# Aggregation by graph: 64-row TensorE tiles in pairs instead of one block-diagonal 128-row matmul

## Chip, cores, metric

One core of one Trainium2 chip. The metric is the device time of one launch in microseconds (us). Every ratio is between kernels run in the same rounds on the same chip. A difference between two experiments can cross rounds and chips; the medians of the kernel before in all these rounds lie between 2644.3 and 2645.0.

## The reference, cut to what matters

128 graphs of 64 nodes with 256 features pass through four layers. The first is a five-step gated network, which is most of the time; each of its steps sums the neighbours' features (`agg`):

```python
A = (adj != 0).astype(x.dtype)                    # (128, 64, 64)
for l in range(5):
    m = jnp.einsum('bnd,de->bne', h, weight[l])
    agg = jnp.einsum('bij,bid->bjd', A, m)        # the aggregation
    h = _gru_cell(agg, h, w_ih, w_hh, b_ih, b_hh)
# layer 1: neighbour sum again, then a two-layer MLP; layers 2 and 3: other uses of adj
```

The kernel aggregates `h` first and multiplies by the weights after, which is the same sum. All arithmetic is f32.

## The kernel before

Two graphs are stacked on the 128 partitions and four such pairs ("blocks", NB = 4) make a group, so there are 16 groups. The adjacency of a block is a 128 x 128 tile `ed[:, b, :]` with one graph in each diagonal quarter and zeros elsewhere. One aggregation handles 128 of the 256 features: four matmuls into one PSUM bank (PSUM holds matmul results; the program has eight banks) and one copy of the bank by ScalarE. There are 16 groups x 6 (five steps and layer 1) x 2 feature halves = 192 aggregations.

```python
# layer 0, step l, feature half c   (cut)
ps = bank("ps_agg")
for b in range(NB):
    def one(ps=ps, b=b, c=c, l=l, hr=hr):
        h = hr[:, b, :] if l else xt[:, b, c * P:(c + 1) * P]
        matmul(ps[:, b * P:(b + 1) * P], h, ed[:, b, :], 0, 1)   # out, stationary, moving
    pe(128, one, [ps], [hr if l else xt, ed])
act(512, lambda ps=ps, a=agg[c]: nc.scalar.copy(a.tile(), ps.tile()), [agg[c]], [ps])
```

`pe`, `act` and `flow.op` only record an operation with a guessed duration. At the end, `Flow.issue` puts the operations of up to five streams (set-up and groups) in one static order by list scheduling, so that other groups' work fills the waits of one. The guesses therefore decide the order, but they are not times.

Of the kernel before, what the change touches and what calls it, by code (L numbers as in the profile page):

```python
# [16 lines left out]
P = 128  # L17
# [25 lines left out]
class Op:  # L43
    __slots__ = ("eng", "us", "run", "stream", "n", "need", "then", "at", "bufs", "opens")

    def __init__(self, eng, us, run, stream, n):
        self.eng, self.us, self.run, self.stream, self.n = eng, us, run, stream, n
        self.need, self.then, self.at, self.bufs, self.opens = 0, [], 0.0, (), None


class Flow:
# [18 lines left out]
    def op(self, eng, us, run, w=(), r=()):  # L70
        o = Op(eng, us, run, len(self.streams) - 1, len(self.ops))
        before = set()
        for accesses, writes in ((r, False), (w, True)):
            for a in accesses:
                b, part = a if isinstance(a, tuple) else (a, None)
                if not b.uses and b.slot is not None:
                    ring = self.slots.setdefault(b.slot[0], deque(maxlen=b.slot[1]))
                    if len(ring) == b.slot[1]:
                        before.update(u[0] for u in ring[0].uses)
                    ring.append(b)  # L80
                for u, p, wr in b.uses:
                    if (wr or writes) and (p is None or part is None or p == part):
                        before.add(u)
        before.discard(o)
        touched = set()
        for accesses, writes in ((r, False), (w, True)):
            for a in accesses:
                b, part = a if isinstance(a, tuple) else (a, None)
                if b.bank and not b.uses:
                    o.opens = b  # L90
                b.uses.append((o, part, writes))
                if b not in touched:
                    touched.add(b)
                    b.left += 1
        o.bufs = [b for b in touched if b.bank]
        o.need = len(before)
        for u in before:
            u.then.append(o)
        self.ops.append(o)

    def issue(self):
        clock = dict.fromkeys(self.AHEAD, 0.0)
        queues = [{e: deque(o for o in ops if o.eng == e) for e in clock} for ops in self.streams]
        banks = [0.0] * BANKS
        left = sum(len(ops) for ops in self.streams)
        first = 0
        while left:
            best = None
            for s in range(first, min(first + 5, len(queues))):
                for e, q in queues[s].items():  # L110
                    opened = False
                    for i, o in zip(range(self.AHEAD[e]), q):
                        if o.opens is not None and (opened or not banks):
                            opened = True
                            continue
                        if o.opens is not None and o.need:
                            opened = True
                        if o.need:
                            continue
                        t = max(clock[e], o.at, banks[0] if o.opens is not None else 0.0)  # L120
                        if best is None or (t, s, o.n) < best[0]:
                            best = (t, s, o.n), o
            (t, s, _), o = best
            queues[s][o.eng].remove(o)
            o.run()
            end = t + o.us
            clock[o.eng] = end
            if o.opens is not None:
                banks.pop(0)
            for u in o.then:  # L130
                u.need -= 1
                u.at = max(u.at, end + (self.HOP if u.eng != o.eng else 0.0))
            for b in o.bufs:
                b.left -= 1
                if not b.left:
                    banks.append(end + self.HOP)
                    banks.sort()
            left -= 1
            while first < len(queues) and not any(queues[first].values()):
                first += 1  # L140
# [3 lines left out]
def kernel(  # L144
# [29 lines left out]
    nc = tc.nc  # L174
    B, N, D = x.shape
# [3 lines left out]
    NB = 4  # L179
# [13 lines left out]
    flow = Flow()  # L193
    quads = [slice(t * N, (t + 1) * N) for t in range(2)]
# [5 lines left out]
    def bank(name):  # L200
        return Buf(lambda: psum.tile([P, 512], F32, tag="bank", name=name), bank=True)
# [7 lines left out]
    def matmul(o, lhsT, rhs, k, nk):  # L209
        nc.tensor.matmul(o, lhsT, rhs, start=(k == 0), stop=(k == nk - 1))  # L210

    def pe(n, run, w, r):
        flow.op("PE", {512: 0.86, 256: 0.46, 257: 0.46, 128: 0.33}.get(n, 0.3), run, w, r)
# [7 lines left out]
    def act(n, run, w, r):  # L221
        flow.op("ACT", 0.16 + 0.001 * n, run, w, r)
# [122 lines left out]
    for l in range(L):  # L345
        ps = bank("ps_wmT")
# [8 lines left out]
        for k in range(KD):  # L355
            for j, n in ((0, 2 * D), (2 * D, D)):
                ps = bank("ps_wmih")
# [38 lines left out]
    def group(g):  # L396
# [12 lines left out]
        def rows_T(tag, name, bufs, src):  # L409
# [7 lines left out]
                act(R, lambda ps=ps, k=k: nc.scalar.copy(dst[k].tile(), ps.tile()), [dst[k]], [ps])  # L417
            return dst

        def layer_norm(y, name):  # L420
            st, mv = tiny("st", (P, NB, 6)), tiny("mv", (P, NB, 2))
            ve, rstd = tiny("ve"), tiny("rstd")
            for b in range(NB):
                dve(256, lambda b=b: nc.vector.bn_stats(st[:, b, :], y[:, b, :]), [(st, b)], [(y, b)])  # L424
                dve(4, lambda b=b: nc.vector.bn_aggr(mv[:, b, :], st[:, b, :]), [(mv, b)], [(st, b)])  # L425
            pool(0.23, lambda: nc.gpsimd.tensor_scalar(ve.tile(), mv[:, :, 1], LN_EPS, None, OP.add), [ve], [mv])  # L426
            pool(1.04, lambda: nc.gpsimd.tensor_tensor(rstd.tile(), ve.tile(), m_half, OP.pow), [rstd], [ve])  # L427
            o = rows("xn", f"x_{name}", 2)
            for b in range(NB):
                dve(256, lambda b=b: nc.vector.tensor_scalar(  # L430
                    o[:, b, :], y[:, b, :], mv[:, b, 0:1], rstd[:, b:b + 1], OP.subtract, OP.mult),
                    [(o, b)], [(y, b), mv, rstd])
            return o
# [3 lines left out]
        xt = loads.pop(g)  # L437
        araw, ed = a_raw[s], edge[s]
        for t in range(2):
            q = quads[t]  # L440
            dve(128, lambda q=q: nc.vector.tensor_scalar(ed[q, :, q], araw[q, :, q], 0.0, None, OP.not_equal),
                [(ed, t)], [(araw, t)])
        ps = bank("ps_adjT")
# [8 lines left out]
        hr = None  # L452
        for l in range(L):
            agg = [u("agg", f"agg{l}_{c}", bufs=2) for c in range(KD)]
            for c in range(KD):
                if l:
                    hr = u("hr", f"hr{l}_{c}", (P, NB, P), 2)
                    ps = bank("ps_hr")
                    for b in range(NB):
                        turn(lambda ps=ps, b=b, h=hT[c]: nc.tensor.transpose(  # L460
                            ps[:, b * P:(b + 1) * P], h[:, b * P:(b + 1) * P], ident.tile()), [ps], [hT[c]])
                    act(512, lambda ps=ps, hr=hr: nc.scalar.copy(hr.tile(), tiles_of(ps.tile())), [hr], [ps])
                ps = bank("ps_agg")
                for b in range(NB):
                    def one(ps=ps, b=b, c=c, l=l, hr=hr):
                        h = hr[:, b, :] if l else xt[:, b, c * P:(c + 1) * P]
                        matmul(ps[:, b * P:(b + 1) * P], h, ed[:, b, :], 0, 1)
                    pe(128, one, [ps], [hr if l else xt, ed])
                act(512, lambda ps=ps, a=agg[c]: nc.scalar.copy(a.tile(), ps.tile()), [agg[c]], [ps])  # L469
            hN = [u("hT", f"hT{l}_{c}", bufs=4) for c in range(KD)]  # L470
            for c in range(KD):
                def gate(i, sides, name):
# [38 lines left out]
        for h in range(NB // 2):  # L511
            ps = bank("ps_h")
            for k in range(KD):
                for j in range(2):
                    b = 2 * h + j
# [3 lines left out]
            for j in range(2):  # L519
                b = 2 * h + j  # L520
# [5 lines left out]
        for t in range(2):  # L526
            q = quads[t]
# [3 lines left out]
        x1 = layer_norm(y0, "n0")  # L531


        agg = [u("agg", f"aggm{c}", bufs=2) for c in range(KD)]
        for c in range(KD):
            ps = bank("ps_agg1")
            for b in range(NB):
                pe(128, lambda ps=ps, b=b, c=c: matmul(
                    ps[:, b * P:(b + 1) * P], x1[:, b, c * P:(c + 1) * P], ed[:, b, :], 0, 1), [ps], [(x1, b), ed])
            act(512, lambda ps=ps, a=agg[c]: nc.scalar.copy(a.tile(), ps.tile()), [agg[c]], [ps])  # L540
        hid = [u("hT", f"hid{c}", bufs=4) for c in range(4)] + [u("hr", f"hid{4 + c}", (P, 3 * D), 2) for c in range(2)]
        hid += [u(t, f"hid_{t}") for t in "AB"]
        hid = hid[:KH]
# [2 lines left out]
        for c in range(KH):  # L546
            ps = bank("ps_hid")
# [15 lines left out]
        ps = bank("ps_ss")  # L563
# [13 lines left out]
        for c in range(KH):  # L577
# [4 lines left out]
            b, i = (gt[0], None) if c % 3 == 0 else (gt[1], c % 3 - 1)  # L582
# [7 lines left out]
        for h in range(NB // 2):  # L590
            ps = bank("ps_o1")
            for j in range(2):
                b = 2 * h + j
# [4 lines left out]
            for j in range(2):  # L598
                b = 2 * h + j
# [40 lines left out]
        for h in range(NB // 2):  # L640
            for j in range(2):
                b = 2 * h + j
                pe(256, lambda b=b, j=j, ps=sup[h]: matmul(
                    ps[:, j * D:(j + 1) * D], adjT[:, b, :], tan[:, b, :], 0, 1), [sup[h]], [adjT, (tan, b)])
            for j in range(2):
                b = 2 * h + j
# [110 lines left out]
```

## Time and profile before

| | before |
|---|---|
| time, median (range), 3 runs | 2644.6 us (2644.04 to 2645.34) |
| PE busy / span of the profiled run | 2563.2 / 2642.7 us |
| pairs of weight load and matmul | 8770, of them 1536 in the aggregation |
| mean granted TensorE clock | 0.988 |

An f32 matmul stands in the trace as two pairs of LDWEIGHTS (on PEld; it loads the stationary operand) and MATMUL (on PE; it streams the columns of the moving operand). A matmul's listed duration (276 ns) is its latency; its pace is the distance from one start to the next. Since PE is busy 97% of the time, a change is judged by what it does to PE's pace.

### The profile page before, as it was taken

The numbers are of one execution on the slowest core, as the hardware profiler recorded it, in microseconds if no ns is written. First come the engines' busy times: TensorE is split into PE (matmuls) and PEld (weight loads), VectorE is DVE, ScalarE is ACT, GpSimd is POOL, SyncE is SP. The second block draws the span as 40 slices with busy tenths as digits, with TensorE's granted clock in tenths as the row PEclk, the third lists the DMA queues.
The fourth block names the chain that finished last, engine by engine and source line by source line (L and its number), as shares of the span: only waits on it lengthen the run. The fifth ranks groups of instructions, "written<-read, shape, count | busy, mean of one in ns | idle before, by whom it ended". The sixth has DMA issues, their size and how long they took to land.

```text
span 2642.7 us, 24329 instructions
## 1 busy us (share of the span) xinstructions
PE 2563.2 (97%) x8770; PEld 1448.5 (55%) x8770; DVE 1312.2 (50%) x3191; ACT 933.4 (35%) x1637; POOL 321.5 (12%) x374
## 2 busy tenths in 40 slices
PE   6999999999999999999999999999999999999974
PEld 4556555464655556565565655546465564655543
DVE  1335455463555535455464555536455463545535
ACT  2334333342433334333343433334333333433321
POOL 1002010100202002020110202011020200202010
PEclk9999999999999999999999999999999999999986
DMA  4000000000000000000000000000000000000000
GB/s 120 3 0 10 9 3 17 0 11 8 3 16 3 16 0 11 9 3 16 3 9 8 11 8 3 17 0 11 8 1 16 1 8 9 1 9 1 8 0 8
DMA packets 30696, 26.24 MB, mean 10 GB/s; under 512 B 9668, under 2 KB 30176, under 8 KB 30576
## 3 DMA queue, kind: packets, MB, share of 16 engines
q1 hardware_dynamic: 26416, 19.67, 2.4%
q10 hardware_dynamic: 3760, 4.46, 0.6%
q8 instruction: 69, 1.13, 0.2%
q0 software_dynamic: 400, 0.57, 0.1%
q14 instruction: 51, 0.42, 0.1%
HBM read 16.30 MB, written 8.39 MB: 9 GB/s over the span
## 4 chain that ended last, share of the span: by engine, by line
PE 89%; DVE 5%; ACT 2%; POOL 1%; DMA 1%; issue 1%; POOLq 0%; DVEq 0%; SPq 0%; ACTq 0%
PE p_r L210 19%; PE p_z L210 19%; PE p_hn L210 10%; PE p_in L210 10%; PE ps_o L210 9%; PE ps_hid L210 8%; PE ps_agg L210 5%; PE ps_a L210 2%; PE ps_hr L460 2%; PE ps_wmih L210 1%; PE ps_T L415 1%; PE ps_att L210 1%; DVE st L424 1%; PE ps_sup L210 1%; POOL rstd L427 1%
## 5 line engine op out<-in xcount | busy, mean ns | idle before, releaser
L210 PE MATMUL p_r<-hT,whhT 128*128 128x512 f32 x640 | 311.8, 593 | 0.0
L210 PE MATMUL p_r<-agg,wmih 128*128 128x512 f32 x640 | 304.6, 593 | 0.9 <-ACT agg L469 0.9
L210 PE MATMUL p_hn<-hT,whhT 128*128 128x512 f32 x640 | 305.1, 592 | 0.0
L210 PE MATMUL p_in<-agg,wmih 128*128 128x512 f32 x640 | 304.9, 592 | 0.0
L210 PE MATMUL p_z<-agg,wmih 128*128 128x512 f32 x640 | 304.8, 593 | 0.0
L210 PE MATMUL p_z<-hT,whhT 128*128 128x512 f32 x640 | 304.4, 592 | 0.0
L495 DVE SCALAR_TENSOR_TENSOR A<-A,B 128x512 f32<-128x512 f32 x160 | 114.4, 715 | 360.0 <-ACT B L493 359.6
L498 ACT ACTIVATE A<-A,cols 128x512 f32<-128x512 f32 x160 | 115.5, 722 | 319.6 <-DVE A L497 319.6
L210 PE MATMUL ps_hid<-aggm,w1s 128*128 128x512 f32 x512 | 223.6, 595 | 0.2 <-ACT aggm L540 0.2
L491 ACT ACTIVATE A<-p_r,half_b 128x512 f32<-128x512 f32 x160 | 109.7, 686 | 313.8 <-PE p_r L210 252.9
L501 ACT ACTIVATE B<-p_z,half_b 128x512 f32<-128x512 f32 x160 | 109.6, 685 | 304.2 <-PE p_z L210 304.1
L426 POOL TENSOR_SCALAR ve<-mv 128x4 f32<-128x4 f32 x64 | 19.0, 297 | 1622.4 <-DVE mv L425 1622.4
L504 DVE SCALAR_TENSOR_TENSOR C<-B,C 128x512 f32<-128x512 f32 x160 | 113.9, 712 | 178.3 <-ACT B L501 175.3
L210 PEld LDWEIGHTS p_r<-agg,wmih 128*128 128x128 f32 x640 | 118.5, 190 | 136.5 <-issue 133.2
L210 PEld LDWEIGHTS p_z<-hT,whhT 128*128 128x128 f32 x640 | 119.6, 190 | 133.9 <-issue 130.6
L210 PEld LDWEIGHTS p_in<-agg,wmih 128*128 128x128 f32 x640 | 119.7, 190 | 133.5 <-issue 130.6
L210 PEld LDWEIGHTS p_hn<-hT,whhT 128*128 128x128 f32 x640 | 119.0, 190 | 132.2 <-issue 124.4
L210 PEld LDWEIGHTS p_z<-agg,wmih 128*128 128x128 f32 x640 | 119.6, 190 | 130.9 <-issue 129.6
L210 PE MATMUL ps_o<-w2s,hid 128*128 128x256 f32 x768 | 182.8, 384 | 5.1 <-DVE hid L587 5.1
L210 PEld LDWEIGHTS ps_o<-w2s,hid 128*128 128x128 f32 x768 | 146.9, 193 | 40.8 <-issue 9.1
L500 DVE TENSOR_TENSOR C<-hT,A 128x512 f32<-128x512 f32 x160 | 118.1, 738 | 97.0 <-ACT A L498 97.0
L210 PEld LDWEIGHTS p_r<-hT,whhT 128*128 128x128 f32 x640 | 112.6, 191 | 95.0 <-issue 91.1
(160 smaller groups left out, 3245.4 us busy)
## 6 DMA issues: line engine op xcount, KB each, us to landing
x<-in_x_dram SPq DMA_DIRECT2D x16, 512.0 KB, 3.9
out_dram<-x_n SPq DMA_DIRECT2D x16, 512.0 KB, 2.9
a_raw<-in_adj_dram SPq DMA_DIRECT2D x32, 64.0 KB, 2.5
wm<-in_L_gnn_weight_dram ACTq DMA_DIRECT2D x5, 256.0 KB, 7.0
w1s<-in_L_gnn_W_dram ACTq DMA_DIRECT2D x1, 1024.0 KB, 11.2
w2s<-in_L_gnn_W_dram ACTq DMA_DIRECT2D x1, 1024.0 KB, 11.2
raw_ih<-in_L_gnn_w_ih_dram ACTq DMA_DIRECT2D x3, 256.0 KB, 5.3
raw_hh<-in_L_gnn_w_hh_dram SPq DMA_DIRECT2D x3, 256.0 KB, 6.8
```

What stands on the lines that cost most here:

```text
L210: nc.tensor.matmul(o, lhsT, rhs, start=(k == 0), stop=(k == nk - 1))
L415: turn(lambda ps=ps, b=b, k=k: nc.tensor.transpose(ps[:, b * P:(b + 1) * P], src[:, b, k * P:(k + 1) * P], ident.tile()), [ps], [(src, b)])
L424: dve(256, lambda b=b: nc.vector.bn_stats(st[:, b, :], y[:, b, :]), [(st, b)], [(y, b)])
L426: pool(0.23, lambda: nc.gpsimd.tensor_scalar(ve.tile(), mv[:, :, 1], LN_EPS, None, OP.add), [ve], [mv])
L427: pool(1.04, lambda: nc.gpsimd.tensor_tensor(rstd.tile(), ve.tile(), m_half, OP.pow), [rstd], [ve])
L460: turn(lambda ps=ps, b=b, h=hT[c]: nc.tensor.transpose(ps[:, b * P:(b + 1) * P], h[:, b * P:(b + 1) * P], ident.tile()), [ps], [hT[c]])
L491: act(512, lambda p=p_r, t=ta, c=c: nc.scalar.activation(t.tile(), p.tile(), AF.Tanh, bias=half_b[:, c:c + 1], scale=0.5), [ta], [p_r, hal ...
L495: dve(512, lambda t=ta, v=tb: nc.vector.scalar_tensor_tensor(t.tile(), t.tile(), 1.0, v.tile(), OP.add, OP.mult), [ta], [ta, tb])
L498: act(512, lambda t=ta, i=i_n: nc.scalar.activation(t.tile(), t.tile(), AF.Tanh, bias=bih(i)), [ta], [ta, cols])
L500: dve(512, lambda d=tc_, h=hc, t=ta: nc.vector.tensor_sub(d.tile(), h.tile(), t.tile()), [tc_], [hc, ta])
L501: act(512, lambda p=p_z, z=tb, c=c: nc.scalar.activation(z.tile(), p.tile(), AF.Tanh, bias=half_b[:, KD + c:KD + c + 1], scale=0.5), [tb], ...
L504: dve(512, lambda d=tc_, z=tb: nc.vector.scalar_tensor_tensor(d.tile(), z.tile(), 1.0, d.tile(), OP.add, OP.mult), [tc_], [tc_, tb])
```

## The change

Intent: the zero quarters need not be multiplied. Each 128 x 128 block becomes two matmuls, one per graph, with 64 rows of contraction and 64 moving columns. The two lie in different row halves of the array and can run beside each other. Each half writes a bank of its own, so an aggregation takes two banks and two copies of 256 columns. The four blocks are one operation for the scheduler.

```diff
+        def aggregate(dst, src, c):
+            ps = [bank("ps_agg") for _ in range(2)]
+            def both():
+                for b in range(NB):
+                    for t, q in enumerate(quads):
+                        matmul(ps[t][:, b * N:(b + 1) * N], src[q, b, c * P:(c + 1) * P], ed[q, b, q], 0, 1)
+            flow.op("PE", 1.1, both, ps, [src, ed])
+            for t in range(2):
+                act(256, lambda t=t: nc.scalar.copy(
+                    dst.tile().rearrange("p (b t n) -> p b t n", t=2, n=N)[:, :, t, :],
+                    ps[t][:, :NB * N].rearrange("p (b n) -> p b n", n=N)), [(dst, t)], [ps[t]])
 ...
-                ps = bank("ps_agg")
-                for b in range(NB):
-                    def one(...): ...
-                    pe(128, one, [ps], [hr if l else xt, ed])
-                act(512, ...)
+                    aggregate(agg[c], hr, 0)       # for l > 0; aggregate(agg[c], xt, c) for l = 0
 ... (the same in layer 1; the scheduler learns to open two banks for one operation)
```

More of the change, by code (lines that the diff above doesn't have):

```diff
@@ L47, in __init__ @@
         self.eng, self.us, self.run, self.stream, self.n = eng, us, run, stream, n
-        self.need, self.then, self.at, self.bufs, self.opens = 0, [], 0.0, (), None
+        self.need, self.then, self.at, self.bufs, self.opens = 0, [], 0.0, (), 0
 class Flow:
@@ L89, in op @@
                 if b.bank and not b.uses:
-                    o.opens = b
+                    o.opens += 1
                 b.uses.append((o, part, writes))
@@ L112, in issue @@
                     for i, o in zip(range(self.AHEAD[e]), q):
-                        if o.opens is not None and (opened or not banks):
+                        if o.opens and (opened or len(banks) < o.opens):
                             opened = True
                             continue
-                        if o.opens is not None and o.need:
+                        if o.opens and o.need:
                             opened = True
@@ L119, in issue @@
                             continue
-                        t = max(clock[e], o.at, banks[0] if o.opens is not None else 0.0)
+                        t = max(clock[e], o.at, banks[o.opens - 1] if o.opens else 0.0)
                         if best is None or (t, s, o.n) < best[0]:
@@ L127, in issue @@
             clock[o.eng] = end
-            if o.opens is not None:
-                banks.pop(0)
+            del banks[:o.opens]
             for u in o.then:
@@ L462, in group @@
                     act(512, lambda ps=ps, hr=hr: nc.scalar.copy(hr.tile(), tiles_of(ps.tile())), [hr], [ps])
-                ps = bank("ps_agg")
-                for b in range(NB):
-                    def one(ps=ps, b=b, c=c, l=l, hr=hr):
-                        h = hr[:, b, :] if l else xt[:, b, c * P:(c + 1) * P]
-                        matmul(ps[:, b * P:(b + 1) * P], h, ed[:, b, :], 0, 1)
-                    pe(128, one, [ps], [hr if l else xt, ed])
-                act(512, lambda ps=ps, a=agg[c]: nc.scalar.copy(a.tile(), ps.tile()), [agg[c]], [ps])
+                    aggregate(agg[c], hr, 0)
+                else:
+                    aggregate(agg[c], xt, c)
             hN = [u("hT", f"hT{l}_{c}", bufs=4) for c in range(KD)]
@@ L535, in group @@
         for c in range(KD):
-            ps = bank("ps_agg1")
-            for b in range(NB):
-                pe(128, lambda ps=ps, b=b, c=c: matmul(
-                    ps[:, b * P:(b + 1) * P], x1[:, b, c * P:(c + 1) * P], ed[:, b, :], 0, 1), [ps], [(x1, b), ed])
-            act(512, lambda ps=ps, a=agg[c]: nc.scalar.copy(a.tile(), ps.tile()), [agg[c]], [ps])
+            aggregate(agg[c], x1, c)
         hid = [u("hT", f"hid{c}", bufs=4) for c in range(4)] + [u("hr", f"hid{4 + c}", (P, 3 * D), 2) for c in range(2)]
```

## The prediction

> **What bounds the kernel now.** I read the page first: busy shares, slices, the chain that ended last. Then four equal stretches of the steady part, then the timeline around one aggregation, because the question is what sets the pace of its matmuls.
>
> ```profile
> PE 2563.2 (97%) x8770; PEld 1448.5 (55%) x8770; DVE 1312.2 (50%) x3191; ACT 933.4 (35%) x1637; POOL 321.5 (12%) x374
> PEclk9999999999999999999999999999999999999986
> PE 89%; DVE 5%; ACT 2%; POOL 1%; DMA 1%; issue 1%; POOLq 0%; DVEq 0%; SPq 0%; ACTq 0%
> ```
>
> PE is the bound: busy 97% of the span, 89% of the chain, at full granted clock. The next view (500 us stretches: span of it, then busy us per engine) says the same of the middle, where PE has under 2.5 us of idle in 500. So whatever the change adds to or takes from PE time goes nearly one for one into the end; ACT and DVE have half their time free.
>
> ```profile
> 800.00:1300.00 500.00, 497.65 (x1688) 277.65 (x1687) 254.02 (x612) 179.85 (x313) 58.58 (x66) 1.00 0.02 8
> 1300.00:1800.00 500.00, 498.51 (x1745) 283.51 (x1744) 261.93 (x630) 186.98 (x327) 72.53 (x78) 1.00 0.03 8
> ```
>
> The aggregation is the three ps_agg groups on PE (by form): 1024 + 256 + 256 = 1536 records. The kernel calls 192 banks x 4 matmuls = 768, so each f32 matmul is two LDWEIGHTS+MATMUL pairs in the trace. 1536 pairs of 8770, 207 us of busy union.
>
> ```profile
> L210 PE MATMUL ps_agg<-edge,hr 128*128 128x128 f32 x1024 | 137.4, 276 | 4.3 <-ACT hr L462 4.0
> L210 PE MATMUL ps_agg<-edge,x 128*128 128x128 f32 x256 | 37.0, 278 | 0.0
> L210 PE MATMUL ps_agg<-edge,x_n 128*128 128x128 f32 x256 | 32.7, 283 | 5.1 <-DVE x_n L430 5.1
> ```
>
> The mean of 276 ns is latency, not pace. The pace is in the timeline (start, length, engine, what): one whole bank is 8 pairs, and then 8 pairs with a moving operand of only one column (ps_ss).
>
> ```profile
> 1003.33 0.97 PEld L210 LDWEIGHTS ps_agg<-edge,hr 128*128 128x128 f32 x8
> 1003.44 1.06 PE L210 MATMUL ps_agg<-edge,hr 128*128 128x128 f32 x8
> 1004.33 0.27 PE L415 MATMUL ps_T<-ident,x 128*128 128x128 f32 x1
> ...
> 1004.56 0.97 PEld L210 LDWEIGHTS ps_ss<-ones,sqs 128*128 128x128 f32 x8
> 1004.67 0.95 PE L210 MATMUL ps_ss<-ones,sqs 128*128 128x1 f32 x8
> ```
>
> The bank starts at 1003.44 and the next work at 1004.33: 0.89 us for 8 pairs, 111 ns each. The ps_ss pairs stream 1 column where the bank streams 128, and their 8 loads still take the same 0.97 us, 111 ns apart ((0.97 - 0.19) / 7). This is the most important reading: **with 128 stationary columns the weight load alone sets a pace of about 110 ns per pair, however few columns are streamed.** The 512-column matmuls show what streaming costs: two start 0.86 us apart per two pairs, so 0.84 ns per column and about 107 ns for 128. In the aggregation load and stream are equal.
>
> **What the Trainium skill says.** (1) "TensorE: Matmul & The Clock Gate", section LDWEIGHTS: a load takes its number of columns / 1.2 ns, and the row count makes no difference. For 128 columns that is an estimate of 107 ns; the trace's 111 ns agrees, and the one 64-row load in the program (ps_nm, below) is no shorter, 0.18 us against 0.19. (2) "TensorEngine Tiling (Array Packing)", section Tiling Modes: tiles are independent, and different tiles can load weights and multiply in parallel. No run yet shows it: nothing in this trace is a pair of row tiles. (3) The same section: changing the tiling mode drains TensorE. The trace has one place for it, ps_nm, and agrees (below). (4) The same page, section Restrictions and Gotchas: row tiles write to different PSUM banks and may not use one at the same time, which is why the change takes two banks per aggregation.
>
> **The change part by part.**
>
> *Matmuls.* Each block's 128x128 block-diagonal matmul becomes two, one per graph: 64 rows of contraction, 128 stationary columns, 64 moving columns. So 1536 matmuls and 3072 pairs instead of 1536. Streaming halves per pair (64 x 0.84 = 54 ns, an estimate from the 512-column pace). The zeros off the diagonal are no longer multiplied: that is the intended gain, up to half of 1536 x 111 ns = 170 us. But the stationary operand keeps its 128 columns, so every pair still needs a load of about 110 ns, and there are twice as many loads.
> - If loads to the two row halves run beside each other: 1536 slots x 111 ns = 170 us, exactly as before. No gain, because load and not stream is then the limit.
> - If they follow each other: 3072 x 111 = 341 us, 171 us more.
>
> *Mode switches.* In the static order of the changed kernel's PE instructions the 192 aggregations stand in 154 runs between other work (120 of one aggregation, 30 of two, 4 of three). Each run goes into 64-row mode and out of it. The cost is read at ps_nm, the only 64-row matmul between 128-row ones:
>
> ```profile
> 13.38 0.42 PE L415 MATMUL ps_T<-ident,x 128*128 128x128 f32 x1
> 13.73 0.18 PEld L318 LDWEIGHTS ps_nm<-ident,nmr 64*128 64x128 f32 x1 [0.33 <-issue]
> 13.73 0.37 PE L318 MATMUL ps_nm<-ident,nmr 64*128 64x64 f32 x1
> 14.03 0.71 PEld L445 LDWEIGHTS ps_adjT<-ident,a_raw 128*128 128x128 f32 x4
> ```
>
> Elsewhere a load starts some 0.11 us before its matmul (1003.33 and 1003.44); here both loads wait until their matmul's turn, at 13.73 and again at 14.03: nothing is pulled ahead across a switch. From the last ps_T at 13.38 to 14.03 is 0.65 us for two matmuls. At that stretch's pace (8 ps_T from 11.84 to 13.38, so 0.22 each) they would take 0.33 to 0.44. So a way in and out costs 0.21 to 0.32 us, on a clock that had not warmed up; I take 0.25. 154 x 0.25 = 39 us, all of it on PE, all on the path.
>
> *Copies.* 192 ScalarE copies of 128x512 become 384 of 128x256. The trace has both widths out of PSUM:
>
> ```profile
> L469 ACT COPY agg<-ps_agg 128x512 f32<-128x512 f32 x160 | 93.1, 586 | 169.8 <-PE ps_agg L210 169.7
> L362 ACT COPY wmih<-ps_wmih 128x256 f32<-128x256 f32 x10 | 3.7, 372 | 2.8 <-PE ps_wmih L210 2.8
> ```
>
> 2 x 372 - 586 = 158 ns more per aggregation, 30 us in all on an engine that is 35% busy. The gates' first use of agg comes 0.16 us later; PE waited for agg for only 0.9 us in the whole run, as the order puts other groups' work in between. I count 0 to 3 us.
>
> *Banks.* An aggregation now needs two free banks of eight before it may start. PE's waits on readers of PSUM are not among its longest (those are one-off waits at start and end), so I count 0 to 5 us.
>
> Sum with parallel loads: 0 + 39 + 0 to 8 = about 2644.6 + 42 = 2687 us, 1.6% slower. Where I chose: 0.25 us per run, and that loads pair up.
>
> **The rivals.**
> - *Loads serialise* (chance about 0.27). For: both halves' loads come from one instruction stream, and in this trace loads never start closer than about 110 ns. Against: every load seen so far covers all 128 rows, so they could not have overlapped, and the skill's statement (2). Then 2645 + 171 + 39 = 2855 us.
> - *Loads pair only in part* (about 0.18): each matmul is two pairs on the same half before the other half's two, so a neighbour is free to overlap only at the borders of two. If a third of the gain of pairing is lost, +57 + 42: about 2745 us.
> - *A gain* (about 0.08): if a 64-row load were really cheaper, or if the pace of the aggregation is set by streaming and not by loads, pairs of 54 ns would save up to 85 us; less 39 for switches is 2600 us. Against: ps_ss keeps 111 ns with one streamed column.
> - *Loads pair fully, switches of another size* (about 0.47): at 0.15 us a run 2668, at 0.35 2700.
>
> **Range and chances.** The gain takes the lowest 8%, full pairing the next 47% (2660 to 2705), partial pairing up to 2760, serial loads the top. The median of this mixture lies near the upper end of full pairing: 2705 us, range 2640 to 2865. Slower by over 2% (above 2697.5) is serial, partial, and a small part of full pairing: 0.52. Within 2%: 0.40. Faster by over 2% (below 2591.7): 0.08.
>
> **What would show it.** In the changed profile, an aggregation's 16 pairs: about 0.9 us from first matmul to last start if loads pair, 1.8 if they follow each other, under 0.6 if I misjudged the load as the limit. LDWEIGHTS starts of the two halves should coincide (64*128 tiles). Each run should show a load that is not pulled ahead at both ends and some 0.1 us of extra gap at each. PE should stay at 96 to 98% busy; the copies should be about 372 ns. The prediction is wrong in kind if PE gains long waits for banks or for agg, or if the gate matmuls change their 0.43 us pace.

## The result, and the profile after

| | before | after |
|---|---|---|
| time, median (range), 4 runs | 2644.97 us (2644.04 to 2645.71) | 2682.37 us (2680.69 to 2683.21) |
| span - PE busy | 79.5 us | 71.0 us |
| pairs in all / in the aggregation | 8770 / 1536 | 10306 / 3072 |
| mean granted clock | 0.988 | 0.988 |

The ratio is 1.0141 (95% interval 1.0123 to 1.0158): 37 us or 1.4% slower, within the 2% band. Ratios are the mean time of one kernel's fast runs over that of the other's of the same rounds, so not quite the ratio of the medians quoted.

The page of the changed kernel: busy time, granted clock, chain.

```profile
PE 2610.4 (97%) x10306; PEld 1452.4 (54%) x10306; DVE 1319.3 (49%) x3191; ACT 951.0 (35%) x1829; POOL 327.9 (12%) x374
PEclk9999999999999999999999999999999999999986
PE 94%; DVE 4%; DMA 1%; POOL 1%; ACT 0%; issue 0%; POOLq 0%; DVEq 0%; SPq 0%; ACTq 0%
```

PE is still the bound, at the same clock. Its idle time (span less busy) fell by 8.5 us, and its busy time rose by 47.2 (2610.4 - 2563.2): new waits are not the loss.

The groups of aggregation matmuls, by form:

```profile
L209 PE MATMUL ps_agg<-edge,hr 64*128 64x64 f32 x2048 | 140.2, 277 | 1.8 <-ACT hr L477 1.8
L209 PE MATMUL ps_agg<-edge,x 64*128 64x64 f32 x512 | 37.6, 287 | 7.4 <-DVE cols L315 7.4
L209 PE MATMUL ps_agg<-edge,x_n 64*128 64x64 f32 x512 | 33.7, 284 | 5.1 <-DVE x_n L445 5.1
```

There are twice as many pairs, and the busy union is almost what it was (211.5 us against 207.1). So the doubled pairs do overlap. Where the 47 us went is seen in the timeline of PE around one aggregation between gate matmuls, and then of PEld in the same place:

```profile
461.21 1.02 PE L209 MATMUL p_r<-hT,whhT 128*128 128x512 f32 x2
462.16 1.11 PE L209 MATMUL ps_agg<-edge,hr 64*128 64x64 f32 x16
463.20 1.13 PE L209 MATMUL p_r<-hT,whhT 128*128 128x512 f32 x2
464.16 1.02 PE L209 MATMUL p_r<-agg,wmih 128*128 128x512 f32 x2
```

```profile
462.16 0.97 PEld L209 LDWEIGHTS ps_agg<-edge,hr 64*128 64x128 f32 x16 [0.76 <-issue]
463.20 0.30 PEld L209 LDWEIGHTS p_r<-hT,whhT 128*128 128x128 f32 x2
```

Sixteen loads take 0.97 us, exactly what eight took before: the loads of the two halves run beside each other. But at 462.16 and at 463.20 the load starts when its matmul is due, not 0.1 us ahead. Compare the distances of starts with those of the control of experiment 1, which has the same order (but for one moved transpose) with 128-row matmuls and so no change of mode:

```profile
453.79 1.02 PE L209 MATMUL p_r<-hT,whhT 128*128 128x512 f32 x2
454.65 1.05 PE L209 MATMUL ps_agg<-edge,hr 128*128 128x128 f32 x8
455.54 1.02 PE L209 MATMUL p_r<-hT,whhT 128*128 128x512 f32 x2
456.40 1.45 PE L209 MATMUL p_r<-agg,wmih 128*128 128x512 f32 x3
```

| from | to | control | changed | more |
|---|---|---|---|---|
| the two p_r before | ps_agg | 0.86 us | 0.95 us | 0.09 |
| ps_agg | the next p_r | 0.89 | 1.04 | 0.15 |
| that p_r pair | the following one | 0.86 | 0.96 | 0.10 |

A way into and out of 64-row mode costs 0.34 us here. The last 0.10 is easy to miss: the recorded start of the first matmul after the switch is the start of its load, so the exposed load shows only in the distance to the matmul after it. Where a transpose comes next instead of a gate matmul, that last step is 0.06 and the sum 0.30 (medians of the trace).

What an aggregation costs inside the mode is seen where two stand in one run:

```profile
678.47 2.00 PE L209 MATMUL ps_agg<-edge,x_n 64*128 64x64 f32 x32
680.40 1.12 PE L209 MATMUL p_z<-hT,whhT 128*128 128x512 f32 x2
```

Thirty-two pairs take 1.93 us to the next start and 16 take 1.04, so the second aggregation takes 0.89 us, as in the control. The row tiles make good the doubling exactly; the loss is at the borders.

### The profile page after: what moved, and what is told of

Same layout as the page of the kernel before. It is cut to its first block, busy times and chain, and to the rows that moved or that the text cites. A ratio compares the mean times of both kernels' runs of the same rounds, so it can differ in the third digit from the quotient of the medians.

```text
span 2681.4 us, 27580 instructions
## 1 busy us (share of the span) xinstructions
PE 2610.4 (97%) x10306; PEld 1452.4 (54%) x10306; DVE 1319.3 (49%) x3191; ACT 951.0 (35%) x1829; POOL 327.9 (12%) x374
## 4 chain that ended last, share of the span: by engine, by line
PE 94%; DVE 4%; DMA 1%; POOL 1%; ACT 0%; issue 0%; POOLq 0%; DVEq 0%; SPq 0%; ACTq 0%
PE p_r L209 21%; PE p_z L209 19%; PE p_hn L209 10%; PE p_in L209 10%; PE ps_o L209 8%; PE ps_hid L209 8%; PE ps_agg L209 7%; PE ps_a L209 2%; PE ps_hr L475 2%; PE ps_sup L209 1%; PE ps_wmih L209 1%; PE ps_T L414 1%; PE ps_att L209 1%; DVE st L439 1%; DVE C L515 1%; PE ps_ss L209 1%
## 5 line engine op out<-in xcount | busy, mean ns | idle before, releaser
L441 POOL TENSOR_SCALAR ve<-mv 128x4 f32<-128x4 f32 x64 | 25.0, 390 | 1612.9 <-DVE mv L440 1612.9
```

What stands on the lines that cost most here:

```text
L441: pool(0.23, lambda: nc.gpsimd.tensor_scalar(ve.tile(), mv[:, :, 1], LN_EPS, None, OP.add), [ve], [mv])
```

## The experiments

Theory: loads of 128 columns set the pace at about 111 ns; row tiles let two loads run together, which just pays for there being twice as many; what is lost is the drain and the exposed load at each of 154 runs of aggregations. Rivals: the loss comes from the new order, the two banks or the longer copies; row tiles do nothing for the loads; streaming sets the pace.

### 1. The order without the mode

```diff
-                    for t, q in enumerate(quads):
-                        matmul(ps[t][:, b * N:(b + 1) * N], src[q, b, c * P:(c + 1) * P], ed[q, b, q], 0, 1)
+                    matmul(ps[b // 2][:, (b % 2) * P:(b % 2 + 1) * P], src[:, b, c * P:(c + 1) * P], ed[:, b, :], 0, 1)
```
(and each copy takes the two blocks of its bank)

> The changed kernel with the order of its operations, its two banks and its two 256-column copies per aggregation, but the 128-row, 128-column matmuls of before: no 64-row mode, so none of the 154 ways in and out of it. If the mode switches are the whole loss (236 ns per run of aggregations in the trace, 154 runs, 36 us), this takes 2645 us, within 5 of the kernel before. If the loss comes from the order, the one-piece aggregation, the two banks or the longer copies, it stays at 2670 to 2682.

Measured: 2637.21 us, ratio to before 0.9972 (0.9957 to 0.9987), correct. It is not at 2645 but 7 under it, so the rest of the change is a small gain, and the 64-row mode costs 45.2 us (2682.4 - 2637.2), more than the whole loss: 0.293 us for each of 154 runs. The traces find it where the theory puts it: from the matmul before a run to the second one after it, the changed kernel takes longer than this control by 45.2 us, summed over the 154 runs, waits included. The rival with order, banks and copies falls.

### 2. The doubled pairs without row tiles

```diff
-                        matmul(..., src[q, b, c * P:(c + 1) * P], ed[q, b, q], 0, 1)
+                        matmul(..., src[:, b, c * P:(c + 1) * P], ed[:, b, q], 0, 1)
```

> The changed kernel with the same 3072 load and matmul pairs, 64 streamed columns each, but 128-row operands (the zero half included): the same result and order, no row tiles, no mode switches. If a load of 128 columns sets a pace of 111 ns and row tiles only make up for there being twice as many, the loads now follow each other: 2682 - 36 + 1536 x 0.111 = 2816 us. If the row tiles did nothing for the pace: about 2646. If the stream of 64 columns set the pace: about 2646 too, or less.

Measured: 2800.61 us, ratio 1.0591 (1.0575 to 1.0607), correct. That is 163.4 us above experiment 1 for 1536 more pairs, 106 ns each, though each streams half as many columns. In its timeline 16 pairs of one aggregation take 1.74 us to the next start:

```profile
481.86 1.89 PE L209 MATMUL ps_agg<-edge,hr 128*128 128x64 f32 x16
483.60 1.08 PE L209 MATMUL p_r<-hT,whhT 128*128 128x512 f32 x2
```

The 2816 expected was some 15 too high: 9 because experiment 1 lies under 2646, 7 because a pair costs 106 ns and not 111. Without row tiles the doubling would cost 163 us; with them, as shown above, an aggregation inside the mode costs no more than before.

### 3. Sixteen columns streamed instead of 64 (wrong result on purpose)

```diff
-                        matmul(ps[t][:, b * N:(b + 1) * N], ..., ed[q, b, q], 0, 1)
+                        matmul(ps[t][:, b * N:b * N + 16], ..., ed[q, b, t * N:t * N + 16], 0, 1)
```
(the copies repeat the 16 columns four times; the order came out slightly different, 157 runs)

> Wrong result on purpose: each 64-row matmul streams 16 columns instead of 64, and the copies repeat them; loads, pairs, tiles, copies as in the changed kernel (157 runs of aggregations instead of 154). If the load sets the pace, nothing changes: 2682 us within 4, 112 ns from one pair of tiles to the next. If streaming has a part in it, the time falls, by up to 3072 / 2 x 40 ns = 60 us.

Measured: 2724.61 us (2712.48 to 2733.77), ratio 1.0287, mean granted clock of the profiled run 0.968 instead of 0.988. The time was a miss. The pace is as the theory has it; 16 loads still take 0.97 us:

```profile
464.60 0.97 PEld L209 LDWEIGHTS ps_agg<-edge,hr 64*128 64x128 f32 x16 [0.76 <-ACT A L503]
```

What was not expected is that the clock falls to half for stretches of 3.4 to 10.2 us, although PE is busy all the while: 99 us in all between 45 and 2500 us. At half pace they cost up to 49 us, about the whole 51 by which the profiled run (2733.8) exceeds the changed kernel. Its view by stretches (span, then busy PE, PEld, DVE, ACT, POOL, and the granted clock), and the p_r matmuls there, 3.65 us for four where four at full clock take 1.9:

```profile
224.00:228.00 4.00, 4.00 (x39) 3.46 (x36) 1.22 (x2) 1.95 (x6) 0.21 (x1) 0.63 0.00 0
228.00:232.00 4.00, 4.00 (x11) 1.99 (x12) 3.04 (x6) 2.21 (x5) 0.00 (x0) 0.52 0.00 0
```

```profile
226.67 1.89 PE L209 MATMUL ps_agg<-edge,hr 64*128 64x16 f32 x16
228.49 3.65 PE L209 MATMUL p_r<-hT,whhT 128*128 128x512 f32 x4
```

### 4. Is that the data or the stream? (wrong result on purpose)

The changed kernel's matmuls with experiment 3's copies, so the same wrong data follow.

```diff
-                        matmul(ps[t][:, b * N:b * N + 16], ..., ed[q, b, t * N:t * N + 16], 0, 1)
+                        matmul(ps[t][:, b * N:(b + 1) * N], ..., ed[q, b, q], 0, 1)
```

> Wrong result on purpose: streams 64 columns as the changed kernel does, but copies only 16 of each 64 and repeats them, so that the data that follow are as wrong as in the run with 16 streamed columns (2725 us, mean granted clock 0.968 instead of 0.988). If that lower clock came from streaming few columns, this takes 2682 us at 0.988; if from the data, 2725 at 0.968.

Measured: 2681.67 us, ratio 1.0139, clock 0.988. So it is not the data. The order is another rival, as experiment 3's differs in places from this run's. But at 709.7, 1365.1 and 2013.6 us of experiment 3 the clock falls in PE work that this run does in the same order, also three times (from 681.5, 1320.9 and 1960.3 us), each time at full clock. The gate matmuls that follow at the first of these places, in experiment 3 and here (clock 1.00 from 696 to 710 us):

```profile
715.37 3.62 PE L209 MATMUL p_r<-hT,whhT 128*128 128x512 f32 x4
704.27 1.88 PE L209 MATMUL p_r<-hT,whhT 128*128 128x512 f32 x4
```

At these places the number of streamed columns is what differs. It is not the only way to a lower clock: the changed kernel has one such stretch (3.4 us at 1821 us), experiment 6 below has four. In the stretch shown above, the one-column ps_ss and transposes lie beside the aggregations; what it takes in general was not tested.

### 5. Shorter loads: four 64 x 64 tiles

```diff
-                        matmul(ps[t][:, b * N:(b + 1) * N], src[q, b, c * P:(c + 1) * P], ed[q, b, q], 0, 1)
+                        for s in range(2):
+                            d = slice(c * P + s * N, c * P + (s + 1) * N)
+                            matmul(ps[t][s * N:(s + 1) * N, b * N:(b + 1) * N], src[q, b, d], ed[q, b, q], 0, 1)
```

> 64 stationary columns as well: four tiles of 64 x 64, each graph's two halves of the features into the two halves of its bank; twice as many pairs (6144), each with a load half as long. If the load's columns set the pace and four tiles run beside each other, a group of four takes 56 ns, an aggregation 0.45 us instead of 0.89, and the time is 2682 - 192 x 0.445 = 2597 us, 1.8% under the kernel before. If column tiles do not load beside each other, 2682. If the rate of instructions is the limit (28 ns per load or matmul on average in the changed kernel), an aggregation takes 1.8 us: 2850.

Measured: 2619.19 us, ratio 0.9905 (0.989 to 0.992), correct: faster than before, though 22 us short of the estimate. The loads and the aggregation in its timeline:

```profile
453.18 0.56 PEld L209 LDWEIGHTS ps_agg<-edge,hr 64*64 64x64 f32 x32 [0.76 <-issue]
```

```profile
453.18 0.69 PE L209 MATMUL ps_agg<-edge,hr 64*64 64x64 f32 x32
453.81 1.13 PE L209 MATMUL p_r<-hT,whhT 128*128 128x512 f32 x2
```

Thirty-two loads in 0.56 us: four tiles load together, and the load's columns set the pace. From the aggregation's start to the next is 0.63 us instead of 1.04, 192 x 0.41 = 79 us less by this one place. PE's idle time, though, rose to 86.5 us (2619.4 - 2532.9) from 71.0. That makes the 63 us gained. Of the 22 us missed, 15 are waits that the estimate left out; the rest is that an aggregation became 0.41 us shorter and not 0.445.

### 6 and 7. More switches, by themselves

One 128-row transpose into unused columns of the bank, in the middle of each aggregation or at its end.

```diff
                         matmul(ps[t][:, b * N:(b + 1) * N], src[q, b, c * P:(c + 1) * P], ed[q, b, q], 0, 1)
+                    if b == 1:                 # experiment 6; b == NB - 1 in experiment 7
+                        nc.tensor.transpose(ps[0][:, 3 * P:], ident.tile(), ident.tile())
```

> The changed kernel with one 128-row transpose into unused columns added in the middle of each aggregation: 346 runs in 64-row mode instead of 154, and 192 transposes of 0.11 us. To be compared with the next run, which has the same transposes at the end of each aggregation (192 runs). If a way in and out costs 290 to 340 ns (as the two traces show it, counted to the second matmul after a run), this is 192 x 0.29 = 56 us above the next run; if it costs the 0.25 us that was predicted, 48; if switching is free and the loss has another cause, 0.

> The control: the same 192 transposes, at the end of each aggregation, so that every aggregation is a run of its own (192 runs instead of 154). 2682 + 192 x 0.11 + 38 x 0.29 = 2714 us if switches cost 0.29; 2703 if they are free.

Measured: 2769.12 us (ratio 1.0469) and 2712.33 us (1.0254), both correct. The work is the same, with 346 runs in the mode against 192. That is 154 more; the 192 x 0.29 of the expectation is a slip, and 154 x 0.29 would be 45 us. Measured are 56.8 us, 0.37 each. Part of this is the clock: it stands at half for 27 us between 45 and 2500 us in experiment 6 and for 10 in experiment 7, worth up to 8.5 us. The other 48 are 0.31 each. The control came to within 2 us of the expected 2714.

### 8 and 9. Fewer switches

Both feature halves in one operation with four banks: 96 runs instead of 154; and the same with 128-row matmuls as its control.

```diff
-        def aggregate(dst, src, c):
+        def aggregate(dsts, srcs, cs):
-            ps = [bank("ps_agg") for _ in range(2)]
+            pss = [[bank("ps_agg") for _ in range(2)] for _ in dsts]
             def both():
-                for b in range(NB):
+                for ps, src, c in zip(pss, srcs, cs):
+                    for b in range(NB): ...
-            flow.op("PE", 1.1, both, ps, [src, ed])
+            flow.op("PE", 2.2, both, pss[0] + pss[1], srcs + [ed])
```

> The changed kernel with both feature halves aggregated in one piece (four banks at once): 96 runs in 64-row mode instead of 154. If a switch costs 0.29 us, 58 fewer give 17 us: 2665 us, give or take what the new order does; against the control of the next run 96 x 0.29 = 28 us more. If the loss were in the doubled pairs or the copies, nothing changes: 2682, and 45 us above the control.

> The control for the run before: the same one piece, four banks and copies, with 128-row, 128-column matmuls and no switches. 2637 us within 8 if the larger piece costs nothing in waits; 10 us more or above if holding four banks or waiting for both transposes stalls TensorE.

Measured: 2680.23 us (1.0133) and 2647.32 us (1.0009), both correct; for the first, 2665 had been expected. The 64-row mode costs 32.9 us here, 0.343 for each of 96 runs; the price falls with the number of runs, as the theory says, though each is a little dearer than estimated: after 91 of these runs comes a gate matmul, the costlier case above (0.34 us), against 88 of 154 in the changed kernel. The larger piece itself costs 10 us (2647.3 against 2637.2), most of it new waits for the previous step's result. The first line here is from the control's waits of PE, with total us, times and the longest; such a wait was 3.4 us in all before:

```profile
PE ps_hr L475 <- DVE hT L519: 12.2, 6, 4.4
```

So merging hardly pays for 64-row tiles (2680 against 2682).

### 10. What gained 7 us in experiment 1

The kernel before, with an aggregation's four matmuls as one piece of 1.1 us, one bank and one copy.

```diff
-                    pe(128, one, [ps], [...])            # four operations of 0.33
+            flow.op("PE", 1.1, both, [ps], [src, ed])    # one operation; both() issues the four matmuls
```

> The kernel before with one thing of the change: a half's four 128 x 128 matmuls are one piece for the order (cost 1.1 us), one bank and one 512-column copy as before. The control with the change's order, two banks and two copies took 2637, 7 under before. If handling the aggregation as one piece is what gains, 2637; if the two shorter copies or banks do, 2645.

Measured: 2633.48 us, ratio 0.9956 (0.9939 to 0.9973), correct. The gain comes from the one piece in the order; 8.8 us of it is PE idle time (70.7 us of span less busy, 79.5 before). Whether the single piece or its lower cost guess does it was not separated. Two banks and two copies, and the order that comes with them, then take back 3.7 us (2637.2 - 2633.5, from different rounds whose medians of before differ by 0.2).

### 11. The best version: 64 x 64 tiles, both halves in one piece

> 64 x 64 tiles and both feature halves in one piece: 96 runs in the smaller mode instead of 154. From the run with 64 x 64 tiles (2619): 58 fewer ways in and out at 0.36 us (its trace) save 21, four banks in one piece cost 10 (as between the two 128-row controls): 2608 us. If the larger piece costs more where aggregations are shorter, 2619 or above.

Measured: 2604.50 us, ratio 0.9849 (0.9834 to 0.9863), correct: 40 us faster than the kernel before and 78 faster than the changed one. It lies within 4 us of the estimate.

## Why the prediction was right, point by point

| step | predicted | measured |
|---|---|---|
| doubled pairs and their pairing | 0 (loads pair) | 0: 0.89 us per aggregation in the mode, as in exp. 1 (+ 163.4 without tiles, exp. 2 - exp. 1) |
| 154 ways in and out | + 39 (0.25 us each) | + 45.2 (0.293 each, changed - exp. 1) |
| copies and banks | + 0 to 8 | + 3.7 (exp. 1 - exp. 10) |
| handling as one piece | not foreseen | - 11.3 (exp. 10 - before) |
| sum | + 42, 2687 us | + 37.6; 2682.4 measured |

The last three differences form a chain from the kernel before to the changed one, so they add up to the loss by construction; what tests them is each trace.

- **The mechanism held.** The load of 128 columns is the limit, two row halves load together, nothing is gained, and the switches are the loss. Experiments 1, 2, 5, 6 and 7 each show one part of it. The single most useful reading was ps_ss, where one streamed column cost as much as 128.
- **The switch was sized a seventh too low** (0.25 against 0.293 us). It was read at ps_nm up to the recorded start of the next matmul (14.03). The exposed load of that matmul falls after that start, so it was left out. The slow pace there (0.22 us per ps_T, 0.11 at 1003 us) worked the other way; a clock not warmed up, as the prediction has it, is not shown, as the granted clock reads 1.00 from 11 to 15 us.
- "Every load seen so far covers all 128 rows" overlooked ps_nm (64 rows) and ps_cols (28). Neither has a neighbour in the other rows, so nothing hangs on it.
- **The one-piece order was not seen.** The prediction looked only at what an aggregation costs and did not ask what the new order does to other waits; 11 us less came from it. The two errors nearly cancel, so the good sum is partly luck.
- **The quoted 2705 was a mixture.** It sat above the main theory's 2687 because serial and partial pairing were given 45% together. Both fell. The main theory's own band, 2660 to 2705, held the result; so did the range. Slower than 2% was called the likeliest outcome (0.52) and did not come: 1.4% lies in the band given 0.40.
- Copies of 376 ns and an unchanged gate pace away from switches came as said; long waits for banks did not come.

## What to carry to other kernels

Before splitting a matmul into tiles, ask whether streaming or the weight load sets its pace: splitting rows leaves the load's columns as they are and doubles the loads, so concurrency only pays the debt; splitting columns too shortened the loads and won. Count how many times the order enters and leaves the tile mode, and multiply by a switch cost measured to the second instruction after the switch. And run the new order with the old instructions as a control, since a rewrite can move the schedule by as much as the idea it carries.

## What the Trainium skill lacked or had wrong

- "TensorEngine Tiling (Array Packing)", section Tiling Modes, says that a mode change drains TensorE and that tiles load and multiply in parallel. Both agree with the traces. It gives no cost: a way in and out took 0.29 to 0.34 us in these f32 streams, and at all 154 entries the load started within 2 ns of its matmul, none ahead. It leaves open whether two tiles also load at the same time, which is what counted: 16 loads in 0.97 us as 8 before, 32 of half the columns in 0.56.
- The same page, section Performance Considerations, recommends row tiling wherever the contraction is 64 or less, and its overview gives up to 2x as the theoretical speedup. Where the load is the limit, row tiling of a block-diagonal matmul gave nothing (0.89 us per aggregation in either form without the switches); row and column tiling together halved it (1.09 us for two in a run less 0.63 for one, 0.46, in experiment 5's trace).
- "TensorE: Matmul & The Clock Gate", section Part 1, says that the clock follows how busy PE is. In experiment 3 the profile has PE busy 4.00 of 4.00 us and granted 0.52; with 64 columns streamed instead of 16, the same work in the same order kept 1.00 (experiment 4, at three places). So how many columns are streamed can matter, and not only the profile's busy share; the page's measure of busy may be another.
